# A fused attention and perception kernel: late weights on the GpSimd queue, pixels of blocks 4 to 7 fetched ahead, another tile for the second pair's parts

## The chip, the cores and the metric

The kernel runs on one core of a Trainium2 chip. The metric is the time of one execution on the device in microseconds (us); of the kernel before there are three runs, and one further execution was profiled. The engines are TensorE (PE, with its weight loads as PEld), VectorE (DVE), ScalarE (ACT), GpSimd (POOL) and SyncE (SP), which here only issues DMAs.

## The reference, cut to what matters

Two layers over four images of 64 x 64 pixels with 256 channels, in float32. The first is attention over all 4096 pixels of an image:

```python
q = x @ Wq + bq                 # 32 columns
k = x @ Wk + bk                 # 32 columns
v = x @ Wv + bv                 # 256 columns
energy = jnp.einsum('bnd,bmd->bnm', q, k)
attn = jax.nn.softmax(energy, axis=-1)
x_out = jnp.einsum('bnm,bmc->bnc', attn, v)
out = gamma * x_out.reshape(B, H, W, Cin) + inputs
```

The second layer works on that result:

```python
perceived = conv_general_dilated(x, w_perc, ...) + b_perc      # depthwise 3x3, 3 outputs a channel
hid = gelu(einsum('bphw,dp->bdhw', perceived, w_up1) + b_up1)
dx = einsum('bdhw,cd->bchw', hid, w_up2) + b_up2
h_new = x + dx
return h_new + local_attention(h_new, w_qkv, b_qkv)            # 3x3 window
```

The weights of the second layer (`w_perc`, `w_up1`, `w_up2`, `w_qkv` and their biases) are called the late weights here: nothing uses them before the first layer has finished some pixels.

## The kernel before, in words

An image is cut into 8 blocks of 512 pixels (8 rows); block `s` runs from 0 to 31 over the four images. The main loop has 32 slots. Slot `s` does the first layer's attention for the 512 queries of block `s` against the 8 key blocks of its image, and around that, in a fixed list of jobs, the second layer for blocks some slots behind (`LAG_PERC`, `LAG_HID`, `LAG_ATT`: 2, 3 and 5 slots). The schedule is written by hand: each engine runs its instructions in the order in which the program emits them, and a DMA is issued in that order by the engine whose queue it names.

A slot has 16 points, two for each key block `G`. At the first point of a pair the kernel loads the keys of block `G + 2` (`load_keys`, line 276) and, from slot 1 on, its values, then forms the energies of the following key block (`energy`, 323, four matmuls into one tile `e` of PSUM that has a single buffer). At each point ACT takes the exponential of half the energies (`weight`, 334), the jobs of that point run, and PE multiplies values by the exponentials (`product`, 339); DVE adds the denominators up (`add_up`, 353).

For the first image the keys, queries and values are made while slot 0 runs. `fetch(s)` (214) puts the pixels of block `s` into a tile: blocks 0 to 3 are copied out of the ring `xp` by DVE and ACT, blocks 4 to 7 come by two DMAs each from HBM, issued by SP (237), into tiles that the second layer uses later (`h` for 4 to 6, `lq` for 7). `project_qk(s)` (243) forms queries and keys of the pair of blocks `s` and `s + 1`; ACT writes them from PSUM as a high and a low part into a tile `both` with the tag `st`, of which there is one (253 to 256), and DVE subtracts (257). SP then stores them to `packed` in HBM (269). For block 0 they go straight into `qa` and `ka` as well (268): twelve small DMAs that read the same tile. Every later key block is read back from `packed` by two DMAs (`load_parts`, 212), which SP issues only when the store has landed. `project_v(s, pair)` (287) forms half a block of values; ACT copies them and stores them to `packed_v`.

Slot 0 has its own job list, two entries after every second point:

```python
early_jobs = [lambda: early(4), *projections(3), lambda: early(6)]
early_jobs += [*projections(4)[:2], *projections(5), *projections(6)[:2], *projections(7)]
```

where `early(s)` fetches blocks `s` and `s + 1` and projects that pair at once. `projections(s)` are the value projections of a block, with the pair's qk projection behind them for an even block.

At point 8 of slot 0 the nine loads of the late weights are issued by ACT (1209 to 1222). Their tiles are written once. Between them stand eight subtractions on POOL (`mix_weights`, 544), which prepare sums of the weights in `wmix` and `wmix2`. POOL's program before them is the filling of constants (145 to 180).

The tag `late` has three buffers, used so far only for the perception of block 30, near the end.

Of the kernel before, what the change touches and what calls it, by code (L numbers as in the profile page):

```python
# [16 lines left out]
P = 128  # L17
B, H, W, C = 4, 64, 64, 256
# [4 lines left out]
NB = 512  # L23
# [4 lines left out]
TPB = NB // P  # L28
# [25 lines left out]
def attention_then_perception_kernel(  # L54
# [37 lines left out]
    def unshifted():  # L92
# [6 lines left out]
        def tile_of(shape, tag, name, bufs=1):  # L99
            return pool.tile(shape, F32, tag=tag, name=name, bufs=bufs)  # L100
# [113 lines left out]
        def fetch(s):  # L214

            b, g = divmod(s, NBLK)
            if 2 <= s < NBLK:

                if s == 2:
                    both = tile_of([P, NHC, NB], "hid", "xc_2_3")  # L220
                    staged[2], staged[3] = both[:, :CH], both[:, CH:]
                elif s == NBLK - 1:
                    t = tile_of([P, CH, UP + RB, W], "lq", f"xc_{s}")
                    staged[s] = t[:, :, UP:, :].rearrange("p c h w -> p c (h w)")
                elif s > 3:
                    t = tile_of([P, CH, 2, HALO + RB, KW], "h", f"xc_{s}", 3)
                    staged[s] = t.rearrange("p c a h w -> p (c a h w)")[:, : CH * NB].rearrange(
                        "p (c n) -> p c n", c=CH
                    )
            else:  # L230
                staged[s] = tile_of([P, CH, NB], "xc", f"xc_{s}", 2)
            rows = x[b].rearrange("p c (h w) -> p c h w", w=WP)
            at, of = (slice(r, r + RB) for r in (1 + g * RB, ring(s)))
            for c in range(CH):
                to = staged[s][:, c, :].rearrange("p (h w) -> p h w", w=W)
                if s >= RING:
                    nc.sync.dma_start(out=to, in_=rows[:, c, at, 1 : 1 + W])
                elif c == 0:
                    nc.vector.tensor_copy(to, xv[:, c, of, 1 : 1 + W])
                else:  # L240
                    nc.scalar.copy(to, xv[:, c, of, 1 : 1 + W])

        def project_qk(s):

            ps = bank("m", f"qk_{s}")
            for kin in range(CH):
                for r in range(2):
                    nc.tensor.matmul(
                        ps[2 * r * CQK : 2 * (r + 1) * CQK, :],
                        lhsT=wqk[:, kin].rearrange("p s d -> p (s d)"),  # L250
                        rhs=staged[s + r][:, kin, :], start=(kin == 0), stop=(kin == CH - 1),
                    )
            both = tile_of([P, 2, NB], "st", f"st_{s}")
            high, low = both[:, 0, :], both[:, 1, :]
            nc.scalar.activation(high.bitcast(F32R), ps, AF.Identity, bias=bqk2)
            nc.scalar.activation(low, ps, AF.Identity, bias=bqk2)  # L256
            nc.vector.tensor_tensor(low, low, high, ALU.subtract)
            if s == 0:
                queries[0] = tile_of([P, NB], "qa", "qa_0", 2)
                for G in range(2):  # L260
                    keys[0, G] = tile_of([P, NB], "ka", f"ka_0_{G}", 3)
                for part, G in ((0, 0), (1, 0), (0, 1), (1, 1)):
                    for i in range(2):
                        for to, at, from_ in (
                            (queries[0], 2 * i + part, 0), (keys[0, G], 2 * part + i, 2 * G + 1)
                        )[G:]:
                            rows, of = (slice(j * CQK, (j + 1) * CQK) for j in (at, from_))
                            nc.sync.dma_start(out=to[rows, :], in_=both[of, part, :])
            nc.sync.dma_start(
                out=packed[s // 2].rearrange("a r q d n -> (r q d) a n"), in_=both  # L270
            )
# [15 lines left out]
        def project_v(s, pair, tag="m"):  # L287
            xc = staged[s]
            if s >= NBLK:
                v = tile_of([P, 2, C], "vs", f"vs_{s}_{pair}", 2)  # L290
            else:
                if pair == 0:
                    values[0, s] = tile_of([P, TPB, C], "v", f"v_0_{s}", 3)
                v = values[0, s][:, 2 * pair : 2 * pair + 2, :]
            ps = bank(tag, f"v_{s}_{pair}")
            for i in range(2):
                for kin in range(CH):
                    nc.tensor.matmul(  # L298
                        ps[:, i * C : (i + 1) * C],
                        lhsT=xc[:, kin, bass.ts(2 * pair + i, P)], rhs=wv[:, kin, :],  # L300
                        start=(kin == 0), stop=(kin == CH - 1),
                    )
            nc.scalar.copy(v, ps.rearrange("p (t c) -> p t c", c=C))
            nc.scalar.dma_start(
                out=packed_v[:, bass.ts(2 * s + pair, 2 * C)], in_=v.rearrange("p t c -> p (t c)")
            )
# [776 lines left out]

        fetch(0)
        fetch(1)
        project_v(0, 0, "acc")
        project_qk(0)
        project_v(0, 1, "acc")
        fetch(2)
        fetch(3)  # L1090
        for i in range(2):
            project_v(1, i)
        project_qk(2)
# [10 lines left out]
        combine = combine_steps()  # L1104


        def early(s):
            fetch(s)
            fetch(s + 1)
            project_qk(s)  # L1110

        early_jobs = [lambda: early(4), *projections(3), lambda: early(6)]
        early_jobs += [*projections(4)[:2], *projections(5), *projections(6)[:2], *projections(7)]
        points = 2 * NG
        for slot in range(NSLOT):
# [54 lines left out]
            for point in range(points):  # L1170
                G, half = divmod(point, 2)
                after = slot + (G + 1) // NG, (G + 1) % NG
                if half == 0:
                    ahead = slot + (G + 2) // NG, (G + 2) % NG
                    if ahead[0] < NSLOT:
                        load_keys(*ahead)
                    if 0 < ahead[0] < NSLOT:
                        load_values(*ahead)
                    if G == NG // 2 and slot + 1 < NSLOT:
                        spread_queries(slot + 1)  # L1180
                    if after[0] < NSLOT:
                        energy(*after)
                if after[0] < NSLOT:
                    weight(*after, half)
                for do in jobs[point]:
                    do()
                product(slot, G, half)

                if point == 0:
                    add_up(slot, 0, 0)  # L1190
                if point < points - 1:
                    add_up(slot, *divmod(point + 1, 2))
                else:
                    partial_sums(slot)


                if slot < NSLOT - 1:
                    to = sum(share[: point + 1])
                else:
                    to = min(n_steps, -(-(point + 1) * n_steps // (points - 2)))  # L1200
                    if point < 3:
                        to = min(to, n_mixed // MULT)
                while stepped < to:
                    next(conv, None)
                    stepped += 1
                if slot == 0 and point == NG:

                    next(combine)
                    blqk = loaded(b_lqk, "blqk", queue=nc.scalar)
                    wperc = loaded(w_perc, "wperc", queue=nc.scalar)  # L1210
                    bperc = loaded(b_perc, "bperc", queue=nc.scalar)
                    wup1 = loaded(w_up1, "wup1", queue=nc.scalar)
                    bup1 = loaded(b_up1, "bup1", queue=nc.scalar)
                    wup2 = loaded(w_up2, "wup2", queue=nc.scalar)
                    mix_weights(
                        *blocks_of(wup1, MULT, C), *(wmix[:, i] for i in range(4))
                    )
                    y = blocks_of(wup2, CH, P)
                    mix_weights(*y, wmix2[:, 0], wmix2[:, 1], y[1], wmix2[:, 2])
                    bup2 = loaded(b_up2, "bup2", queue=nc.scalar)  # L1220
                    nc.scalar.dma_start(out=wlv, in_=w_qkv[:, :, 2 * C :])
                    blv = loaded(b_lv.partition_broadcast(P), "blv", [P, C], queue=nc.scalar)
                if nxt and half == 1:
                    for do in nxt[G]:
                        do()
                    if slot and G + 2 < NBLK:
                        fetch(slot + 1 + G + 2)
# [470 lines left out]
```

## Time and profile before

| | us |
|---|---|
| median of 3 runs | 3414.15 (3413.11 to 3414.49) |
| the profiled execution | 3413.88 |
| its span | 3412.2 |
| PE busy | 3367.9 (99%) |
| DVE busy | 2748.3 (81%) |
| ACT busy | 1072.1 (31%) |
| POOL busy | 347.9 (10%) |

The span runs from the first to the last instruction of the profiled execution; 1.7 us of its time lie around it. A busy PE isn't PE at its peak. The costliest group is the product of values and exponentials (line 347), 1833.7 us; the energies (328) take 363.7. The DMA engines are busy 24.9% of the span with what SP issues, 1.6% with what ACT issues; no DMA of POOL is among the queues.

The first slices of the span differ from the rest. In the page's second part, 40 slices of 85 us each, PE has an 8 in the first slice and a 9 in nearly all others.

### The profile page before, as it was taken

The numbers are of one execution on the slowest core, as the hardware profiler recorded it, in microseconds if no ns is written. First come the engines' busy times: TensorE is split into PE (matmuls) and PEld (weight loads), VectorE is DVE, ScalarE is ACT, GpSimd is POOL, SyncE is SP. The second block draws the span as 40 slices with busy tenths as digits, with TensorE's granted clock in tenths as the row PEclk, the third lists the DMA queues.
The fourth block names the chain that finished last, engine by engine and source line by source line (L and its number), as shares of the span: only waits on it lengthen the run. The fifth ranks groups of instructions, "written<-read, shape, count | busy, mean of one in ns | idle before, by whom it ended". The sixth has DMA issues, their size and how long they took to land.

```text
span 3412.2 us, 32824 instructions
## 1 busy us (share of the span) xinstructions
PE 3367.9 (99%) x11678; PEld 2117.8 (62%) x11678; DVE 2748.3 (81%) x4455; ACT 1072.1 (31%) x1344; POOL 347.9 (10%) x541
## 2 busy tenths in 40 slices
PE   8899999999999999999999999999999999999998
PEld 4456666666666666666666666666666666666655
DVE  1378888867888888876788888888688888888895
ACT  2233333233323333333333323333333332333331
POOL 1100011100111101110011111001110111110031
PEclk9999999999999999999999999999999999999999
DMA  4332222243222222234222222223422222222200
GB/s 141 112 100 75 72 77 72 90 133 101 76 81 81 79 68 78 77 96 136 93 72 76 79 81 83 71 74 108 144 70 79 77 76 72 81 88 66 70 13 26
DMA packets 166975, 285.17 MB, mean 84 GB/s; under 512 B 67860, under 2 KB 69140, under 8 KB 166676
## 3 DMA queue, kind: packets, MB, share of 16 engines
q1 hardware_dynamic: 155684, 263.36, 24.9%
q10 hardware_dynamic: 11120, 19.64, 1.6%
q8 instruction: 95, 1.56, 0.2%
q14 instruction: 76, 0.62, 0.1%
HBM read 240.23 MB, written 41.94 MB: 83 GB/s over the span
## 4 chain that ended last, share of the span: by engine, by line
PE 88%; DVE 7%; DMA 3%; SPq 1%; issue 0%; ACT 0%; ACTq 0%; DVEq 0%; POOL 0%
PE acc L347 46%; PE e L328 7%; PE hid_bc L605 5%; PE hid_de L605 4%; PE hid_gf L605 4%; PE lv L918 3%; DVE perc L500 3%; PE lo L1052 3%; PE hid_a L605 2%; DMA ka<-packed 2%; PE v L298 2%; PE s L959 2%; PE dx_cd L557 1%; PE dx_ab L557 1%; PE dx_eg L557 1%; DVE den L361 1%
## 5 line engine op out<-in xcount | busy, mean ns | idle before, releaser
L347 PE MATMUL acc<-p,v 128*128 128x512 f32 x4096 | 1833.7, 594 | 0.6 <-DVE o L412 0.6
L347 PEld LDWEIGHTS acc<-p,v 128*128 128x128 f32 x4096 | 770.5, 190 | 795.0 <-issue 775.7
L500 DVE SCALAR_TENSOR_TENSOR perc<-xp,wperc,perc 128x512 f32<-128x512 f32 (+2 forms) x1554 | 1107.6, 774 | 27.4 <-ACT perc L496 27.3
L336 ACT ACTIVATE p<-e 128x1024 f32<-128x1024 f32 x512 | 523.9, 1024 | 1689.6 <-PE e L328 748.5
L361 DVE TENSOR_TENSOR den<-den,p 128x1024 f32<-128x1024 f32 x480 | 585.7, 1220 | 85.0 <-ACT p L336 83.1
L328 PE MATMUL e<-qa,ka 128*128 128x512 f32 x1024 | 363.7, 477 | 18.4 <-ACT p L336 14.4
L984 POOL TENSOR_TENSOR lp<-lp,near 128x396 f32<-128x396 f32 x60 | 89.2, 1486 | 2427.3 <-ACT lp L979 2427.3
L328 PEld LDWEIGHTS e<-qa,ka 128*128 128x128 f32 x1024 | 189.8, 189 | 148.4 <-issue 102.9
L605 PE MATMUL hid_de<-perc,wmix 128*128 128x256 f32 x720 | 165.2, 379 | 0.0
L605 PEld LDWEIGHTS hid_de<-perc,wmix 128*128 128x128 f32 x720 | 136.8, 190 | 43.7 <-issue 21.5
L506 DVE TENSOR_TENSOR perc<-perc 128x256 f32<-128x256 f32 x360 | 149.8, 430 | 8.2
L628 ACT ACTIVATE hid<-hid,bup 128x512 f32<-128x512 f32 x120 | 80.1, 714 | 219.8 <-DVE hid L612 219.8
L496 ACT ACTIVATE perc<-xp,bperc,wperc 128x512 f32<-128x512 f32 x192 | 145.4, 805 | 1.8 <-DVE xp L418 1.8
L1007 POOL TENSOR_TENSOR lsum<-lsum,lp 128x99 f32<-128x99 f32 (+1 forms) x179 | 124.1, 700 | 11.7
L918 PE MATMUL lv<-wlv,h 128*128 128x256 f32 x520 | 122.4, 379 | 0.0
L298 PE MATMUL v<-wv,xc 128*128 128x256 f32 x512 | 116.7, 380 | 2.9 <-ACT st L256 2.6
L298 PEld LDWEIGHTS v<-wv,xc 128*128 128x128 f32 x512 | 96.9, 190 | 31.0 <-issue 15.1
L1052 PEld LDWEIGHTS lo<-lp,lv 128*128 128x128 f32 x732 | 104.9, 191 | 17.5 <-issue 9.8
L918 PEld LDWEIGHTS lv<-wlv,h 128*128 128x128 f32 x520 | 98.7, 190 | 15.5 <-issue 2.2
L1052 PE MATMUL lo<-lp,lv 128*128 128x99 f32 (+1 forms) x732 | 104.7, 291 | 0.0
L612 DVE TENSOR_TENSOR hid<-hid_bc,hid 128x512 f32<-128x512 f32 x60 | 41.5, 691 | 75.8 <-PE hid_bc L605 75.8
L336 ACT ACT_TABLE_LOAD x60 | 77.0, 1283 | 77.2 <-PE e L328 75.6
(198 smaller groups left out, 3128.4 us busy)
## 6 DMA issues: line engine op xcount, KB each, us to landing
v<-packed_v SPq DMA_DIRECT2D x248, 512.0 KB
ka<-packed SPq DMA_DIRECT2D x508, 128.0 KB
xp<-in_x SPq DMA_DIRECT2D x30, 528.0 KB
xc<-in_x SPq DMA_DIRECT2D x56, 256.0 KB
out<-lo SPq DMA_DIRECT2D x56, 256.0 KB
packed_v<-vs ACTq DMA_DIRECT2D x48, 256.0 KB
packed<-st SPq DMA_DIRECT2D x16, 512.0 KB
qa<-packed SPq DMA_DIRECT2D x62, 128.0 KB
```

The costliest lines, as they stand in the source:

```text
L298: nc.tensor.matmul(ps[:, i * C : (i + 1) * C], lhsT=xc[:, kin, bass.ts(2 * pair + i, P)], rhs=wv[:, kin, :], start=(kin == 0), stop=(kin = ...
L328: nc.tensor.matmul(e[:, j, :], lhsT=key[:, bass.ts(j, P)].bitcast(F32R), rhs=queries[s].bitcast(F32R), start=True, stop=True,)
L336: nc.scalar.activation(p, energies[s, G][:, 2 * half : 2 * half + 2, :], AF.Exp)
L347: nc.tensor.matmul(accs[s][c], lhsT=v[:, 2 * half + i, bass.ts(c, P)], rhs=p[:, i, :], start=(first and i == 0), stop=(G == NG - 1 and hal ...
L361: nc.vector.tensor_tensor(den, den, p, ALU.add)
L496: nc.scalar.activation(acc, win, AF.Identity, bias=bperc[:, half, j : j + 1], scale=wt)
L500: nc.vector.scalar_tensor_tensor(acc, win, wt, acc, ALU.mult, ALU.add)
L506: nc.vector.tensor_tensor(t[:, to, :], t[:, a, :], t[:, b, :], op)
L605: nc.tensor.matmul(ps[:, n * C : (n + 1) * C], lhsT=w(j), rhs=mixes[s, j][:, kind, :], start=(j == 0), stop=(j == MULT - 1),)
L918: nc.tensor.matmul(ps[:, half * C : (half + 1) * C], lhsT=keys_of(s, t, half, kin), rhs=wlv[:, kin, :], start=(kin == 0), stop=(kin == CH ...
L1007: nc.gpsimd.tensor_tensor(to, to, near_ws[block, half][:, t_, of, :], ALU.add)
L1052: nc.tensor.matmul(pv[:, rows, columns(half)], lhsT=lvs[block, t, half][:, bass.ts(c, P)], rhs=near_ws[block, half][:, t, of, :], start=(i ...
```

## The change

Three edits in the first slot and ahead of it. The nine late loads are issued by POOL in place of ACT, at the same place of the program. Block 4 is fetched behind block 1 and block 5 behind block 3, ahead of slot 0; blocks 6 and 7 are fetched together in a job of slot 0, right behind the projection of pair 4. The tile of the second pair (blocks 2 and 3) has the tag `late` in place of `st`.

```diff
-            both = tile_of([P, 2, NB], "st", f"st_{s}")
+            if s == 2:
+                both = tile_of([P, TPB, C], "late", "st_2", 3).rearrange(
+                    "p (a t) c -> p a (t c)", a=2
+                )
+            else:
+                both = tile_of([P, 2, NB], "st", f"st_{s}")
...
         fetch(0)
         fetch(1)
+        fetch(4)
         project_v(0, 0, "acc")
         project_qk(0)
         project_v(0, 1, "acc")
         fetch(2)
         fetch(3)
+        fetch(5)
...
-        def early(s):
-            fetch(s)
-            fetch(s + 1)
-            project_qk(s)
-
-        early_jobs = [lambda: early(4), *projections(3), lambda: early(6)]
+        def fetch_more():
+            fetch(6)
+            fetch(7)
+
+        early_jobs = [lambda: project_qk(4), fetch_more, *projections(3), lambda: project_qk(6)]
         early_jobs += [*projections(4)[:2], *projections(5), *projections(6)[:2], *projections(7)]
...
-                    blqk = loaded(b_lqk, "blqk", queue=nc.scalar)
-                    wperc = loaded(w_perc, "wperc", queue=nc.scalar)
-                    bperc = loaded(b_perc, "bperc", queue=nc.scalar)
-                    wup1 = loaded(w_up1, "wup1", queue=nc.scalar)
-                    bup1 = loaded(b_up1, "bup1", queue=nc.scalar)
-                    wup2 = loaded(w_up2, "wup2", queue=nc.scalar)
+                    blqk = loaded(b_lqk, "blqk", queue=nc.gpsimd)
+                    wperc = loaded(w_perc, "wperc", queue=nc.gpsimd)
+                    bperc = loaded(b_perc, "bperc", queue=nc.gpsimd)
+                    wup1 = loaded(w_up1, "wup1", queue=nc.gpsimd)
+                    bup1 = loaded(b_up1, "bup1", queue=nc.gpsimd)
+                    wup2 = loaded(w_up2, "wup2", queue=nc.gpsimd)
                     mix_weights(
                         *blocks_of(wup1, MULT, C), *(wmix[:, i] for i in range(4))
                     )
                     y = blocks_of(wup2, CH, P)
                     mix_weights(*y, wmix2[:, 0], wmix2[:, 1], y[1], wmix2[:, 2])
-                    bup2 = loaded(b_up2, "bup2", queue=nc.scalar)
-                    nc.scalar.dma_start(out=wlv, in_=w_qkv[:, :, 2 * C :])
-                    blv = loaded(b_lv.partition_broadcast(P), "blv", [P, C], queue=nc.scalar)
+                    bup2 = loaded(b_up2, "bup2", queue=nc.gpsimd)
+                    nc.gpsimd.dma_start(out=wlv, in_=w_qkv[:, :, 2 * C :])
+                    blv = loaded(b_lv.partition_broadcast(P), "blv", [P, C], queue=nc.gpsimd)
```

What each engine's program becomes: SP issues block 4 ahead of the twelve key and query DMAs of block 0, block 5 ahead of the second pair's store, and the key loads of blocks 3 and 4 behind blocks 6 and 7. On PE, ACT and DVE the same instructions stand in another order in slot 0: the qk projection of pair 4 alone in the first gap, the two value projections of block 3 in the second, the qk projection of pair 6 with half of block 4's values in the third, and every later value projection half a gap further back. ACT's program has nine DMA issues fewer, POOL's nine more: six stand directly behind the filling of constants, three behind the subtractions.

## The prediction

> **What bounds the kernel now.** I read the busy times first, then the waits of PE, then the chain of waits over the first 200 us, and last the DMA share by stretches.
>
> ```profile
> PE 3367.9 (99%) x11678; PEld 2117.8 (62%) x11678; DVE 2748.3 (81%) x4455; ACT 1072.1 (31%) x1344; POOL 347.9 (10%) x541
> ```
>
> PE is busy for 99% of the span, so an edit can gain only where PE still stands idle or runs slowly. The change touches the stretch before slot 1, and there PE does stand idle: the waits of PE from 17 to 142 us are
>
> ```profile
> PE e L328 <- ACT p L336: 14.4, 1, 14.4
> PE qk L248 <- DMA xc<-in_x: 8.6, 4, 5.5
> PE v L298 <- ACT st L256: 2.6, 1, 2.6
> ```
>
> Each line is one part of the change: the first is ACT held by the issues of the late weights, the second the pixels of blocks 4 to 7, the third ACT's wait for the tile `st`. The chain (start, duration, what; some pieces left out) shows what they cost, and the price of undisturbed work:
>
> ```profile
> 18.24 3.02 DMA packed<-st
> 21.52 0.69 ACT st L255
> ...
> 33.61 6.62 DMA xc<-in_x
> ...
> 90.39 16.71 DMA ka<-packed
> 107.12 0.62 ACTq L1221
> 107.78 0.60 ACTq L80
> 108.48 1.03 ACT p L336
> 109.56 2.07 PE e L328 x4
> 111.63 8.17 PE acc L347 x16
> 119.80 3.45 PE v L298 x16
> 123.25 0.93 PE e L328 x4
> 124.19 6.87 PE acc L347 x16
> ```
>
> A key block's product costs 6.87, its energies 0.93, two value projections 3.45 (one 1.73), a qk projection 1.92 (the chain at 7.94). After a long idle the same energies took 2.07 and the product 8.17: 2.4 us for a slow clock. In the timeline of PE the eight products of slot 0 start at 25.69, 45.96, 61.94, 73.39, 84.64, 111.43, 124.02 and 131.82, and slot 1's first at 141.42. Gap minus work: 20.27 - 11.45 = 8.8; 15.98 - 11.45 = 4.5; 11.45 - 11.25 = 0.2; 11.25 - 11.25 = 0; 26.79 - 11.25 = 15.5; 12.59 - 11.25 = 1.3. Slot 0 holds **30.3 us** that aren't work. Slots 1 to 31 are left as they are, and what slot 0 gains is kept, since PE bounds what follows.
>
> The DMA queues decide how much of it is real (stretch, its length, busy time of PE, PEld, DVE, ACT, POOL, clock, DMA share, GB/s):
>
> ```profile
> 10.00:21.00 11.00, 9.95 (x44) 6.89 (x43) 1.57 (x3) 3.94 (x7) 2.92 (x11) 1.00 0.72 234
> 21.00:24.00 3.00, 1.16 (x5) 1.06 (x6) 0.69 (x1) 2.48 (x4) 0.00 (x0) 1.00 0.00 0
> ...
> 38.00:40.00 2.00, 1.77 (x2) 0.29 (x2) 0.00 (x0) 0.00 (x0) 0.00 (x0) 0.50 1.09 232
> ...
> 98.00:103.00 5.00, 0.00 (x0) 0.00 (x0) 0.00 (x0) 0.00 (x0) 0.00 (x0) 0.75 0.98 305
> 134.00:139.00 5.00, 5.00 (x15) 2.37 (x14) 0.00 (x0) 1.02 (x1) 0.00 (x0) 1.00 0.14 53
> ```
>
> From 10 to 21 us the engines are already 72% taken. Pixels move at 232 GB/s with all engines busy, weights at 305. The last row is a key load alone, issued at 131.50: 0.14 of 16 engines is two engines, so its 256 KB take 5 us at 53 GB/s, and it still ran at 139: about **7.7 us from issue to landing**, whatever else is idle.
>
> **The change part by part.**
>
> *Tile for the second pair.* ACT waited 5.71 us (to 21.52) for the DMAs that read `st` of pair 0. The qk projection ends at 17.06 and energy 0 at 18.53, so the exponentials that started at 22.67 could start at 18.55, and the first product 4.1 us earlier. Its keys are later, though, by what now goes first on SP. The two issues for block 4 stand ahead of SP's first key issue (10.59); SP is free at 6.83 and two such issues took 2.5 us and 4.1 us at 47.23 and 29.43, so they end at 9.3 to 10.9: at most 0.3 late. Their 0.52 MB (2.2 us at 232 GB/s) drain after the last rows of `xp`, at 11 to 14, while the keys are issued at one per 0.6 us until 15.7: I take 0.6. The weights then run into the load of key block 1 (issued 15.7 to 18.2): 0 to 6.7 us late, and I take 1 us, since only its last packets meet them. First product: 25.69 - 4.1 + 0.6 + 1 = 23.2, **2.5 earlier** (ends: 4.1 earlier, 3.5 later).
>
> *Pixels ahead of their jobs.* This removes the 8.8 and 4.5 us, unless something else is late. What is late next is key block 2, needed after product 0 and the qk projection of pair 4: 23.2 + 6.87 + 1.92 = 32.0. Before it SP has to land the second pair's parts; before, these were issued at 23.54 and landed 4.56 later, at 28.1. Now the engines must also move block 4 and 5 (1.05 MB, 4.5 us) and the two large weights (2.1 MB at 305 GB/s, 6.8 us), 11.3 us in all, ahead of or beside them. The idle share before was 0.28 x 11 = 3.1 from 10 to 21, and 3.0 from 21 to 24: 5.2 us do not fit. So the parts land at 33.3 if everything goes ahead of them and at 26 if the weights go behind (SP reaches them some 2 us earlier than before). Nearest the first end, since the weights are issued some 8 us ahead; of the 0.5 MB issued last I let most (1.5 of 1.7 us) go behind: 31.8. With 7.7 for the load, key block 2 lands at 39.5: **PE waits 7.5** (ends 1.7 and 9). Behind that wait stand product 1 and all later PE work. An idle of 2.58 us left the clock at 1.00, one of 5.52 brought it to 0.50: I add **2.4** for the clock (ends 0 and 2.4).
>
> Then key block 3. It used to be issued ahead of blocks 6 and 7 and now stands behind them on SP, where four such issues took 8.60 and 8.88 us. [...] The parts of pair 4 wait on DVE, behind the landing of `gbv` (28.99 before, some 5 later now) and four additions, so they go at about 39; pixels to 44, keys landed 7.7 later, 51.7. Needed at 39.5 + 0.93 + 8.17 + 3.45 = 52.0. I take **0.5** (ends 0 and 5). Key blocks 4 to 7 have 5 us or more in hand on the same two engines. The qk projections and value projections that the job list moves are the same instructions in other gaps: nothing.
>
> *Weights from GpSimd.* This removes the 15.5 and 1.3 us, which hold ACT's wait of 17.83 for its nine issues and the slow clock behind it. On POOL the issues start at 13.33, where the last fill of `fold` ends; POOL has nothing else to do until 132.28. The three last loads stand behind the eight subtractions of the mixes (106.65 to 119.8 before, 13 us) and are needed two slots later. The trace has no DMA issued by POOL. An issue by ACT took 0.33 to 0.62, the longest POOL instruction here 2.83; four issues cost 2 to 11 us, so the large load starts at 15 to 24.5. Either way its bytes meet the second pair's parts, and that is in the 7.5.
>
> [...]
>
> **Sum.** 30.3 + 2.5 - 7.5 - 2.4 - 0.5 = 22.4 us gained. The profiled execution had a span of 3412.2 and took 3413.88, 1.7 around it; the span becomes 3389.8. That execution is 0.3 below the median of 3414.15, so the median becomes **3391.7 us**. A first use of a POOL queue outside the span: 0 to 2 us, unseen, taken as 0.
>
> **The rivals.**
>
> *The cover holds (0.22).* The parts land early (26 to 28), the keys by 34 to 36: first product 4.1 earlier, waits 2 to 3 and no slow clock. For it: 3 us of DMA share 0.00 at 21 to 24. Against it: 0.72 from 10 to 21. 30.3 + 4.1 - 2.5 = 31.9: 3382.
>
> *The start is jammed, once (0.12).* First product 3.5 late, 9 at key block 2, 5 at key block 3, 2.4 of clock twice: 30.3 - 3.5 - 9 - 5 - 4.8 = 8.0: 3406. For it: 16.71.
>
> *ACT still waits (0.05).* The wait at 107.12 ended with a key load on SP, not with a weight; if ACT's value stores also wait for key loads, the 15.5 stays: 22.4 - 15.5 = 6.9, 3407. Against it: that load was slow only while the weights ran.
>
> *The other side (0.05): slower.* The POOL queue trickles its weights through the two engines that hold every key load, for four gaps on end: each of key blocks 1 to 4 takes 16.7 in place of 7.7, 9 us each, with 2.4 of clock each: 45.6 lost against 30.3 + 4.1: 3425. It decides once the new waits pass 34 us. For it: the one row of 16.71. Against it: 305 GB/s ends the weights in 7 us.
>
> **How the numbers follow.** The forecast has 0.56; its own range is 3385 to 3399, by the ends of the waits. The range for 8 in 10 takes in the first rival and the milder half of the second: **3380 to 3405**. A measurement of this kernel can tell 0.2% (6.8 us) from no change; faster by more is the forecast, the cover and most of the jam and of ACT's wait: 0.90; within it 0.04; slower 0.06.
>
> **What would show it.** ACT's wait of 17.83 gone; no PE wait on pixels; a PE wait of 5 to 9 us on key block 2 before its energies, with a clock of about 0.5 behind it; first product near 23; slot 1's first product near 119 in place of 141.42; POOL's mixes near 25 to 40. Wrong if DMA share stays under 0.8 from 14 to 30, if energies 2 wait under 3 us, or if a later key block is waited for.

## The result, and the profile after

| | before | after |
|---|---|---|
| median | 3414.32 us (4 runs, 3413.11 to 3415.89) | 3393.99 us (4 runs, 3392.17 to 3395.35) |
| ratio | | 0.994 (95% interval 0.9923 to 0.9957) |
| span of the profiled execution | 3412.2 | 3393.6 |
| first product of slot 0 starts | 25.69 | 31.68 |
| first product of slot 1 starts | 141.42 | 122.97 |
| from the one to the other | 115.7 | 91.3 |

The changed kernel is 20.3 us faster by the medians and 18.6 by the spans; its profiled execution, 3395.35 us, was the slowest of its four. The gain lies ahead of slot 1: 141.42 - 122.97 = 18.5, and slots 1 to 31 and the tail keep their lengths within 0.7 us each. Around the span lie 1.75 us (3395.35 - 3393.6), as before, so POOL's new queue costs nothing outside it. The code stands five lines lower now: the energies are line 333, the exponentials 341, the product 352, the value projection 303.

The page of after, busy times and then the new DMA queue (packets, MB, share of 16 engines):

```profile
PE 3364.7 (99%) x11678; PEld 2118.8 (62%) x11678; DVE 2747.1 (81%) x4455; ACT 1074.8 (32%) x1344; POOL 352.1 (10%) x550
...
q0 software_dynamic: 576, 2.53, 0.2%
```

Every engine is busy about as long as before (PE 3.2 us less); what went is idle time. `q0` is POOL's queue with the late weights. The waits of PE from 15 to 125 us (us in total, times, longest):

```profile
PE e L333 <- DMA packed_v<-v: 6.7, 1, 6.7
PE e L333 <- DMA ka<-packed: 3.9, 2, 2.3
PE acc L352 <- DVE o L417: 0.6, 1, 0.6
```

The three waits of before, 14.4 on ACT, 8.6 on pixels and 2.6 on `st`, are gone. Two others took their place, both on key data. Where they stand shows in the timeline of PE (start, duration, instruction, and in brackets the idle time before it and what ended it):

```profile
24.02 2.05 PE L333 MATMUL e<-qa,ka 128*128 128x512 f32 x4 [6.73 <-DMA packed_v<-v]
25.87 5.05 PE L303 MATMUL v<-wv,xc 128*128 128x256 f32 x16
30.56 1.28 PE L333 MATMUL e<-qa,ka 128*128 128x512 f32 x4
31.68 7.03 PE L352 MATMUL acc<-p,v 128*128 128x512 f32 x16
38.64 1.94 PE L248 MATMUL qk<-xc,wqk 128*64 128x512 f32 x8
42.10 1.15 PE L333 MATMUL e<-qa,ka 128*128 128x512 f32 x4 [1.53 <-DMA ka<-packed]
43.10 7.03 PE L352 MATMUL acc<-p,v 128*128 128x512 f32 x16
49.96 3.62 PE L303 MATMUL v<-wv,xc 128*128 128x256 f32 x16
55.90 1.90 PE L333 MATMUL e<-qa,ka 128*128 128x512 f32 x4 [2.32 <-DMA ka<-packed]
...
92.61 7.03 PE L352 MATMUL acc<-p,v 128*128 128x512 f32 x16
103.86 7.03 PE L352 MATMUL acc<-p,v 128*128 128x512 f32 x16
113.38 7.03 PE L352 MATMUL acc<-p,v 128*128 128x512 f32 x16
122.97 7.13 PE L352 MATMUL acc<-p,v 128*128 128x512 f32 x16 [0.55 <-DVE o L417]
```

The first line is energies 0, the first work on keys at all. It stood at 17.36 before; now it waits 6.73 and runs slowly, and so does the value projection behind it: the granted clock is 0.50 from 24.0 to 25.9 us and 0.72 from there to 31.0. The wait's label needs care: energies read `qa` and `ka` and no `packed_v`. A wait for several semaphores carries the name of the last one by the profile, and the DMAs of SP and ACT share eight semaphores here. In the trace's semaphore records the last that these energies wait for is that of the eighth small DMA, which hands over the last part of block 0's keys: issued at 16.07, it lands at 23.93. In kernels shown below the same wait is named `ka<-st`. The sixth and ninth lines are key blocks 2 and 3. From 92.61 on, where ACT used to hold PE for 15.5 us, the products follow each other at 11.25 and at 9.5, which is work alone.

The gaps between the products, less the work in them as in the prediction: 11.42 - 9.72 = 1.7 at key block 2; 14.49 - 11.25 = 3.2 and 12.53 - 11.45 = 1.1 at key block 3 and behind it; none later. With the first product 31.68 - 25.69 = 6.0 later, 12.0 of the 30.3 us are given back, and 18.3 are left.

ACT's side of the tile (timeline of ACT), and the nine issues on POOL (timeline of POOL):

```profile
17.34 0.69 ACT L260 ACTIVATE st<-qk,bqk 128x512 fp32r<-128x512 f32 x1 [1.29 <-PE qk L248]
...
26.11 1.94 ACT L341 ACTIVATE p<-e 128x1024 f32<-128x1024 f32 x2 [7.50 <-PE e L333]
```

```profile
13.21 0.74 POOL L80 DMA_DIRECT2D blqk<-in_b_lqk  x1
...
15.02 0.54 POOL L80 DMA_DIRECT2D wup<-in_w_up  x1
...
16.10 0.54 POOL L80 DMA_DIRECT2D wup<-in_w_up  x1
24.28 1.86 POOL L551 TENSOR_TENSOR wmix<-wup 128x768 f32<-128x768 f32 x1 [7.65 <-DMA wup<-in_w_up]
```

The second pair is written at 17.34, not 21.52: the tile did its part. Then ACT idles 7.50 for energies 0. POOL has issued both `wup` loads, 2 MB, by 16.64; the first and larger one (1536 KB) lands 9.1 after its issue, at 24.1, about when energies 0 start. Two stretches of the windows show the DMA engines then (the last two columns are their share and GB/s):

```profile
14.00:30.00 16.00, 9.27 (x32) 6.32 (x31) 0.69 (x1) 5.02 (x8) 8.27 (x9) 0.79 1.01 320
17.00:19.00 2.00, 0.29 (x2) 0.00 (x0) 0.36 (x1) 1.27 (x2) 0.00 (x0) 1.00 0.61 215
```

From 14 to 30 us the 16 engines are full on the mean (share 1.01). In the trace's packet records from 17 to 19 us POOL's queue starts 35 packets of 12,288 bytes, and of the keys' packets, 2,048 bytes each on SP's queue, not one starts. The engines' share in those 2 us is only 0.61, so a lack of engine time alone doesn't explain that; why the keys' packets stood still is open.

### The profile page after: what moved, and what is told of

Its sections match the earlier page's. It is cut to its first block, busy times and chain, and to the rows that moved or that the text cites. A ratio compares the mean times of both kernels' runs of the same rounds, so it can differ in the third digit from the quotient of the medians.

```text
span 3393.6 us, 32830 instructions
## 1 busy us (share of the span) xinstructions
PE 3364.7 (99%) x11678; PEld 2118.8 (62%) x11678; DVE 2747.1 (81%) x4455; ACT 1074.8 (32%) x1344; POOL 352.1 (10%) x550
## 4 chain that ended last, share of the span: by engine, by line
PE 90%; DVE 7%; DMA 2%; SPq 0%; issue 0%; ACT 0%; ACTq 0%; DVEq 0%; POOL 0%
PE acc L352 47%; PE e L333 7%; PE hid_bc L610 5%; PE hid_de L610 4%; PE hid_gf L610 4%; PE lv L923 3%; DVE perc L505 3%; PE lo L1057 3%; PE v L303 2%; PE hid_a L610 2%; DMA ka<-packed 2%; PE s L964 2%; PE dx_cd L562 1%; PE dx_ab L562 1%; PE dx_eg L562 1%; DVE den L366 1%
## 5 line engine op out<-in xcount | busy, mean ns | idle before, releaser
L1057 PEld LDWEIGHTS lo<-lp,lv 128*128 128x128 f32 x732 | 104.9, 191 | 17.5 <-issue 9.8
L923 PEld LDWEIGHTS lv<-wlv,h 128*128 128x128 f32 x520 | 98.7, 190 | 15.5 <-issue 2.2
```

The costliest lines, as they stand in the source:

```text
L923: nc.tensor.matmul(ps[:, half * C : (half + 1) * C], lhsT=keys_of(s, t, half, kin), rhs=wlv[:, kin, :], start=(kin == 0), stop=(kin == CH ...
L1057: nc.tensor.matmul(pv[:, rows, columns(half)], lhsT=lvs[block, t, half][:, bass.ts(c, P)], rhs=near_ws[block, half][:, t, of, :], start=(i ...
```

## The experiments

Two readings of the lost 12 us stood against each other: that the weights crowd out the first keys (so they should go later), or that what is now ahead on SP, blocks 4 and 5, makes the keys late. A second question was what sets key blocks 2 and 3: the full engines, or a key load that keeps two engines of 16 busy whatever else is idle (a share of 0.14 from 134 to 139 us of the kernel before). Eight kernels were run, in two groups, each timed beside the kernel before on its chip; the table has all. The kernel before has medians of 3413.84 us in the first group (`held`, `act_issues`, `pool_alone`, `keys16`), 3415.4 in the second and 3414.32 beside after, so a difference of 1 to 2 us between two rows says nothing.

| kernel | median, us | ratio, 95% interval | first product | slot 0's length |
|---|---|---|---|---|
| after | 3393.99 | 0.9923 to 0.9957 | 31.68 | 91.3 |
| `held` | 3384.45 | 0.9897 to 0.993 | 24.02 | 91.7 |
| `act_issues` | 3406.97 | 0.9971 to 0.999 | 23.58 | 110.6 |
| `pool_alone` | 3404.53 | 0.9962 to 0.9982 | 31.59 | 100.1 |
| `keys16` | 3382.68 | 0.9893 to 0.9926 | 28.74 | 85.9 |
| `held_keys16` | 3377.05 | 0.9871 to 0.9904 | 24.09 | 86.1 |
| `tile_only` | 3410.58 | 0.9975 to 0.9994 | 22.73 | 116.4 |
| `fetch_only` | 3412.86 | 0.9984 to 1.0003 | 26.71 | 110.7 |
| `keys_first` | 3390.76 | 0.9912 to 0.9945 | 30.91 | 88.2 |

### The weights behind a product: `held`

A copy on POOL that reads the exponentials of point 6 stands ahead of POOL's issues, so that these start at 53.83 and not at 13.21. All else is as in after.

```diff
+                if slot == 0 and point == 6:
+                    hold = const.tile([P, 1], F32, tag="hold", name="hold")
+                    nc.gpsimd.tensor_copy(hold, weights[0, G, half][:, 0, 0:1])
                 if slot == 0 and point == NG:
```

> Theory (the weights crowd out the first keys): with the weights held back on POOL until the exponentials of key block 3 exist, energies 0 no longer wait 6.7 us, the first product starts near 23 in place of 31.68, key block 2 is waited for by some 2 to 4 us, and the time falls by 5 to 9 us: 3385 to 3389. Rival (block 4's pixels ahead of the keys on SP make them late): the first product stays near 31 and the time at 3394.

Measured 3384.45, 9.5 us less than after by the medians and half a us below the range of the theory. The timeline of PE in `held`:

```profile
18.65 1.16 PE L333 MATMUL e<-qa,ka 128*128 128x512 f32 x4 [1.75 <-DMA ka<-st]
19.64 3.62 PE L303 MATMUL v<-wv,xc 128*128 128x256 f32 x16
22.91 1.27 PE L333 MATMUL e<-qa,ka 128*128 128x512 f32 x4
24.02 7.03 PE L352 MATMUL acc<-p,v 128*128 128x512 f32 x16
...
36.03 2.04 PE L333 MATMUL e<-qa,ka 128*128 128x512 f32 x4 [3.11 <-DMA ka<-packed]
37.87 9.16 PE L352 MATMUL acc<-p,v 128*128 128x512 f32 x16
```

Energies 0 wait 1.75 in place of 6.73, and the first product comes 31.68 - 24.02 = 7.66 earlier: 5.37 by the start of energies 0, and 0.86 + 1.42 because energies 0 and the value projections behind them run at full clock (1.00 on the mean of 14 to 30 us). So the weights cost 7.7 us at the start, with block 4's pixels ahead of the keys in both kernels. Slot 0's length stays (91.7 against 91.3): key block 2 is needed earlier and is waited for longer, 3.11 with a slow clock behind it (0.96 on the mean of 28 to 36 us; the energies take 2.04 and the product 9.16), although no weights move any more. What it waits for is in the windows of `held`:

```profile
28.00:36.00 8.00, 4.92 (x16) 1.51 (x15) 4.98 (x6) 2.29 (x3) 0.00 (x0) 0.96 0.11 37
```

The engines are 11% busy. The chain has the last issue of this load and its landing:

```profile
28.48 7.41 DMA ka<-packed
```

It is a key load alone, and 0.11 of 16 engines is about two; with the others idle it still takes 7.4 us.

### Weights back on ACT, the rest kept: `act_issues`

After with the nine loads issued by ACT, as before the change. This leaves tile and pixels, and takes POOL's queue away.

```diff
-                    blqk = loaded(b_lqk, "blqk", queue=nc.gpsimd)
+                    blqk = loaded(b_lqk, "blqk", queue=nc.scalar)
...
```

> The late weights go back to ACT, the other two edits stay. Theory (weights crowd out the first keys): first product near 23, ACT's wait for its issues is back with 12 to 16 us of PE idle at the energies of key block 6: 3398 to 3403. Rival (pixels of block 4 make the keys late): first product near 31 and the ACT wait on top: 3407 to 3411.

The first product came at 23.58, where the theory has it: with tile and pixels and no weights at the start, energies 0 wait only 1.35. The time, 3406.97, missed the theory's numbers and lies by the rival's, whose mechanism, keys late by block 4's pixels, the first product rules out. The waits of PE in `act_issues`, 15 to 125 us:

```profile
PE e L333 <- ACT p L341: 18.6, 1, 18.6
PE e L333 <- DMA ka<-packed: 2.8, 1, 2.8
PE e L333 <- DMA ka<-st: 1.3, 1, 1.3
```

ACT's timeline there:

```profile
75.95 1.02 ACT L341 ACTIVATE p<-e 128x1024 f32<-128x1024 f32 x1 [2.42 <-PE acc L352]
82.44 0.34 ACTq L80 DMA_DIRECT2D blqk<-in_b_lqk  x1
...
91.53 0.33 ACTq L80 DMA_DIRECT2D bup<-in_b_up  x1
98.64 0.62 ACTq L1227 DMA_DIRECT2D wlv<-in_w_qkv  x1
```

ACT's nine issues stretch over 17.5 us here (82.44 to 99.91) and over 17.8 before, but the issues themselves take only 3.8 and 3.9 of them, 0.33 to 0.62 each. Between them ACT waits. In the semaphore records of the kernel before each of its issues waits until the DMA that last used the same semaphore has landed; SP and ACT share eight of them, and the issues at 94.26, 97.03, 99.88 and 107.12 each follow the landing of one of SP's slow key loads, at 94.24, 97.01, 99.86 and 107.10. In `act_issues` the issue at 98.64 follows the landing, at 98.62, of a key load issued at 81.77. The nine issues on POOL use eight other semaphores in after, and each starts where the one ahead of it ends: six from 13.21 to 16.64, three from 36.98 to 38.82. So the change spared ACT waits for key loads more than the work of issuing. PE's value projections ahead of this wait end 12.6 us earlier than before (82.52 against 95.12), ACT is free only 8.5 earlier, and the difference is the growth of the wait, from 14.4 to 18.6. Time gained ahead of this wait is partly lost in it. Whether the wait would go with ACT still issuing but the key loads as in `keys16` below was not tried.

### One part alone: `tile_only`, `fetch_only`, `pool_alone`

The kernel before with one of the three edits each: the `late` tile for the second pair; blocks 4 and 5 ahead and 6 and 7 in a job of their own; the nine loads on POOL.

```diff
+            if s == 2:
+                both = tile_of([P, TPB, C], "late", "st_2", 3).rearrange(
+                    "p (a t) c -> p a (t c)", a=2
+                )
```

> The kernel before with the second pair's parts in the tile of the tail, nothing else. Theory (the pair's keys and the pixels of block 4 follow the store of these parts on SP, so they come earlier by what ACT gains): first product near 21.5 in place of 25.69, the wait for pixels no longer than 5.5 us; 3409 to 3411. Rival (the gain goes into the wait for pixels): 3413 to 3415.

3410.58, as expected: 4.8 us less than before. The first product starts at 22.73, 3.0 earlier than before and 1.2 later than expected: PE now works without a break from 17.35, so that its own wait of 2.6 for `st` was nearly all that could be had. ACT's wait and PE's 14.2 behind it stay.

```diff
+        fetch(4)
...
+        fetch(5)
...
+        early_jobs = [lambda: project_qk(4), fetch_more, *projections(3), lambda: project_qk(6)]
```

> The kernel before with the pixels fetched ahead, weights on ACT, the second pair's parts in st. Theory (the waits for pixels, 13.3 us with their slow clock, turn into 3 to 6 us of waits for key blocks; ACT's waits for st and for the weights' issues stay): 3404 to 3408. Rival (key loads eat all of it): 3412 to 3415.

3412.86: 2.5 less than before, with 1 inside the interval of the ratio. That misses the theory and lies in the rival's range. The waits of PE from 15 to 125 us in `fetch_only` say why:

```profile
PE e L328 <- ACT p L336: 18.7, 1, 18.7
PE e L328 <- DMA ka<-packed: 4.1, 2, 2.5
PE v L298 <- ACT st L256: 2.2, 1, 2.2
```

All 8.6 us of pixel waits are gone, and as much comes back: 4.1 as waits for key blocks, as the theory had it, and 4.3 in the wait on ACT (18.7 against 14.4), which neither theory nor rival had.

```diff
-                    blqk = loaded(b_lqk, "blqk", queue=nc.scalar)
+                    blqk = loaded(b_lqk, "blqk", queue=nc.gpsimd)
...
```

> The kernel before with the weights on POOL, nothing else. Theory (weights crowd out the first keys): ACT's wait is gone (16.8 us gained), the first product moves from 25.69 to 31 or later, the waits for pixels stay: 3402 to 3406. Rival (the weights cost the start nothing): first product near 26, 3397.

3404.53, as expected. The waits of PE from 15 to 125 us in `pool_alone`:

```profile
PE qk L248 <- DMA xc<-in_x: 9.2, 3, 5.5
PE e L328 <- DMA ka<-st: 4.1, 1, 4.1
```

The timeline of PE has the energies in question:

```profile
21.15 2.04 PE L328 MATMUL e<-qa,ka 128*128 128x512 f32 x4 [4.05 <-DMA ka<-st]
```

No fetch stands ahead of the keys here, and still energies 0 wait 4.1, now under their right name, and the first product comes at 31.59. So the weights delay the start by themselves: energies 0 by 3.8 us (21.15 against 17.36 before), and by 5.4 where block 4's pixels stand ahead of the keys too (after against `held`). By the medians the single edits gain 4.8 + 2.5 + 9.3 = 16.6 us and the three at once 20.3; by the spans of the profiled executions 3.2 + 3.9 + 11.3 = 18.4 and 18.6. So it isn't shown that the edits gain more together than alone.

### Key loads in four DMAs: `keys16`

Each load of keys or queries from `packed` is two DMAs whose outermost dimension has two entries. Here it is four DMAs of 32 partitions, all else as in after:

```diff
         for i in range(2):
-            of = part[i : i + 1].to_broadcast([2, CQK, NB]) if which else part
-            nc.sync.dma_start(out=to[2 * i * CQK : 2 * (i + 1) * CQK, :], in_=of)
+            for j in range(2):
+                at = (2 * i + j) * CQK
+                nc.sync.dma_start(out=to[at : at + CQK, :], in_=part[i if which else j])
```

> The changed kernel with every load of keys and queries cut into four DMAs of 32 partitions, so that no DMA has an outer dimension of two. Theory (a key load is slow because it runs on two engines): the load takes 2 to 4 us in place of 8, the waits of 1.53 and 2.32 us for key blocks 2 and 3 and the slow clock behind the second vanish: 3388 to 3390. Rival (the wait is for the landing of the stores and the order on SP): waits stay within 1 us of what they were: 3393 to 3395; twice as many issues on SP could add to it.

3382.68, some 6 us better than expected. Windows of `keys16` around the load of key block 2 (issued 32.35 to 34.09), and PE's timeline there:

```profile
33.00:35.00 2.00, 2.00 (x6) 0.95 (x5) 1.90 (x3) 1.00 (x1) 2.00 (x4) 1.00 0.39 122
```

```profile
37.57 1.19 PE L334 MATMUL e<-qa,ka 128*128 128x512 f32 x4
38.60 7.03 PE L353 MATMUL acc<-p,v 128*128 128x512 f32 x16
```

122 GB/s for 2 us is 244 KB: by that the 256 KB of a key block move in about 2 us, an estimate, not in 7 to 8. Energies 2, at 37.57, start without a wait, so from the first issue, at 32.35, the keys are there within 5.2 us. No energies of slot 0 wait for a key block any more, and slot 0 is 85.9 us long, against 85.4 of pure work (115.7 - 30.3). That also settles key block 3, which waited 2.32 in after. The rest of the gain wasn't foreseen. Slots 7, 15 and 23, where keys of the next image are made, take 135.4 us each in place of 136.6 to 137.8. And the first product is 2.9 earlier, with a wait of 5.1 at energies 0; why is left open, since the first changed load is issued only at 32.35. The load as two DMAs of outer dimension two has 0.11 of the engines in `held`'s row above, about two of 16; as four DMAs of 32 partitions it has 0.39 in the row here, about six. Why the first form keeps to so few was not shown.

### Both: `held_keys16`

```diff
+                    nc.gpsimd.tensor_copy(hold, weights[0, G, half][:, 0, 0:1])
...
+                nc.sync.dma_start(out=to[at : at + CQK, :], in_=part[i if which else j])
```

> The changed kernel with both edits: weights held back on POOL until the exponentials of key block 3 exist, every key load in four DMAs of 32 partitions. Theory (the two costs add: weights ahead of the first keys, key loads on two engines): first product near 24, slot 0 lasts 86 us, its pure work, no PE wait on a key load anywhere after the first; 3377 to 3379. Rival (held weights meet the loads of key blocks 4 to 6 and cost there what they saved): 3381 to 3384.

The hold of `held` and the loads of `keys16`: 3377.05 us (3376.92 to 3377.5), as expected, and the fastest kernel here. The waits of PE over the whole run of `held_keys16`, the longest row:

```profile
PE e L334 <- DMA ka<-st: 1.3, 1, 1.3
```

This is all that is left of slot 0's waits but 0.3: energies 0 at 18.72 for keys that come behind block 4's pixels (17.35 in `tile_only`, without those pixels). Beside the kernel before, 3415.4 on this chip, it gains 38.4 us. Against after the two edits gain 16.9 together, less than the 9.5 + 11.3 = 20.8 of each alone: `keys16` alone already had 2.9 of the first product, which `held` brings too. By the spans 17.8 us are gained: 7.6 at the first product, 5.2 in slot 0 and 4.9 in slots 7, 15 and 23.

### Keys ahead of blocks 6 and 7: `keys_first`

After, with the job that fetches blocks 6 and 7 moved behind the issue of key block 3.

```diff
-        early_jobs = [lambda: project_qk(4), fetch_more, *projections(3), lambda: project_qk(6)]
+        def first_values():
+            fetch_more()
+            project_v(3, 0)
+
+        early_jobs = [
+            lambda: project_qk(4), lambda: None, first_values, lambda: project_v(3, 1),
+            lambda: project_qk(6),
+        ]
```

> The changed kernel with blocks 6 and 7 fetched behind the loads of key block 3 and not ahead of them. Theory (key block 3 was late because four pixel loads stand ahead of it on SP): the wait of 2.32 us and the slow clock behind it go, 3.3 us in all; 3389 to 3392. Rival (it is late because a key load runs on two engines and takes 8 us wherever it stands): the wait stays at 1.5 to 3 us, or the pixels are now late for the projection of pair 6; 3393 to 3396.

3390.76, as expected, though the intervals of the two ratios overlap; the trace has to decide. The timeline of PE at key blocks 2 and 3 in `keys_first`:

```profile
42.40 1.17 PE L333 MATMUL e<-qa,ka 128*128 128x512 f32 x4 [2.59 <-DMA ka<-packed]
43.41 7.03 PE L352 MATMUL acc<-p,v 128*128 128x512 f32 x16
50.27 3.62 PE L303 MATMUL v<-wv,xc 128*128 128x256 f32 x16
53.54 1.28 PE L333 MATMUL e<-qa,ka 128*128 128x512 f32 x4
```

Key block 3 is no longer waited for, and key block 2 is waited for longer, 2.59 against 1.53. In after the two DMAs of key block 3 were issued behind four of pixels, as the timeline of SP has it:

```profile
43.09 3.68 SPq L237 DMA_DIRECT2D xc<-in_x  x4
46.87 2.52 SPq L212 DMA_DIRECT2D ka<-packed  x4
```

So the wait for key block 3 has two causes, its place on SP and its two engines, and removing either is enough (0.3 us is left in `held_keys16`).

## Why the prediction was right, and where it was wrong

**Time, sign and mechanisms.** 3391.7 was predicted and 3394.0 measured, inside the range. The three removals happened as written: ACT's wait, the pixel waits and the tile's wait are gone, and the engines are full from 14 to 30 us (share 1.01). The new costs were of the kind predicted, key data behind the weights, and near in sum: 18.3 us gained against 22.4. But they fell in other places, and two errors of 8 us cancel, so that the number came out so well is in good part luck:

| term, us gained | predicted | measured in after |
|---|---|---|
| slot-0 time that isn't work, removed | 30.3 | 30.3 |
| first product | +2.5 | -6.0 |
| key block 2, wait and clock | -9.9 | -1.7 |
| key block 3 | -0.5 | -4.3 |
| sum | 22.4 | 18.3 |

**The step that failed** is in the tile's part: "The weights then run into the load of key block 1 (issued 15.7 to 18.2): 0 to 6.7 us late, and I take 1 us, since only its last packets meet them." Energies 0 already need `ka` and `qa` of block 0, by the first eight of the same twelve small DMAs. After issues these eight from 10.83 to 16.66, while the large weights start at 15.02; so block 0's own keys met them, and to meet the weights with the last packets was to wait for them: the keys landed at 23.93, the large load at 24.14. The delay of 5.4 (`held` against after) lies within 0 to 6.7; the slow clock behind it, 2.3 more, was not in the step at all. `pool_alone` shows a delay of 3.8 without the pixels, `held` and `act_issues` show it gone.

Two smaller terms of the first product were off as well. The tile was to bring 4.1, by ACT's wait; PE's own wait was 2.6, and `tile_only` brought 3.0. Block 4's pixels were to cost 0.6 and cost 1.3 (energies 0 at 18.65 in `held`, 17.35 in `tile_only`; 18.71 in `fetch_only`, 17.36 before). The term counted the time to move their bytes; in the chain of `held` one of SP's key issues also waits until a pixel DMA of block 4 has landed:

```profile
7.49 7.05 DMA xc<-in_x
...
14.56 0.51 SPq L273
```

So: predicted -4.1 + 0.6 + 1.0 = 2.5 earlier, measured -3.0 + 1.3 + 7.7 = 6.0 later, which is 2.5 beyond the end that was stated.

**Key block 2** was sized as if PE came for it at 32.0. The rule of that term held: the second pair's parts were to land at 31.8, and SP issued the load at 31.85; it was to land at 39.5, and its energies began at 42.10, beside weights. But PE came at 31.68 + 6.87 + 1.92 = 40.5, so most of the wait had already been paid at energies 0. Where the start is free, in `held`, the wait returns: 3.11, and 0.8 + 2.1 of slow clock. The prediction had said what would prove it wrong, a wait under 3 us at energies 2 or a wait for a later key block, and both came: 1.53, and 2.32 for key block 3. It had also named a first product near 23 as a sign of being right, and that came at 31.68.

**Key block 3** was right in mechanism, since the pixels of blocks 6 and 7 on SP delay it (`keys_first`), and short in size: 0.5 taken, 4.3 measured, under its end of 5. Its term gives the pixels some 4.5 us, the author's estimate by 232 GB/s, where the issues had taken 8.60 and 8.88; no run shows what held those up. In after the four took 3.68, and the keys landed 13.1 us after the issue of pair 4's parts (42.67 to 55.76), against 12.7 predicted.

**What the move spared** was less the issues, 3.9 us, than ACT's waits between them, and with them 14.4 us of PE's waiting. The weights' bytes still met the other transfers: before, the key load issued at 90.39 took 16.71 us beside them, and in after they show at energies 0, 6.73 us, where the prediction looked for them at key block 2. And they need not be paid: in `held`, behind the first keys, they cost PE no wait.

**The rivals.** The start jammed by weights did occur, worse than its 3.5, while its waits of 9 and 5 did not follow: one delay covers the next; so the time stayed with the forecast. The cover did not hold: the engines were full, and the parts landed at 31.84, not at 26 to 28. ACT's value stores do wait for key loads, as the third rival feared (ACT idle 2.84 us at 82.34), but PE is not held by it. And nothing trickled: the large load landed 9.1 us after its issue.

## What to carry to other kernels

A transfer that nobody needs soon did best here, once off a busy engine, at a point behind the transfers that somebody waits for (`held`); on an idle engine's queue it started as soon as it could, and that cost 7.7 of the 15.5 us it saved. When an engine seems busy issuing DMAs, look how long the issues themselves take and what each waits for. When several waits stand in one chain, price each new one from where the consumer will then arrive, because a delay paid early covers the next, and a delay removed uncovers it. A load that keeps only two of 16 engines busy is worth reshaping before anything around it is reordered: `keys16` took 11 us off without moving an instruction of PE.

## What the runs showed of the hardware

- **Small packets on one queue stood still beside large ones on another.** In after, from 17 to 19 us, 35 packets of 12 KB start on POOL's queue and none of the 2 KB ones on SP's, with the engines at a share of 0.61; the last of block 0's keys landed at 23.93, 0.2 us ahead of the large load. Whether the size of the packets or the kind of queue does it was not settled.
- **A DMA issue on POOL was short:** 0.54 to 0.74 us each in after, the one of 1.5 MB too (0.54); the longest here is 0.91, in `pool_alone`.
- **Issues on ACT and SP waited for the other engine's DMAs** through shared semaphores: 17.8 us of ACT's time for 3.9 us of issues in the kernel before, and 2.0 us of SP's there for ACT's load of `wqk`.
- **The clock behind short waits varies.** Waits of 2.58 (before), 2.59 (`keys_first`) and 1.53 left the next energies at 1.15 to 1.2 us; 2.32 (after) gave 1.90, at a granted clock of 0.58 from 55.9 to 60 us, and 3.11 (`held`) 2.04, with products of 7.97 and 9.16. After 2.78 in `act_issues` the energies took 1.15 and only the product behind them was slow, 8.72. A wait of 2.48 in `fetch_only` cost nothing. So a wait of 2.3 to 3.1 us cost 0 to 3 us on top in these runs, and none shows what decides it.
